# Five pieces for the third table part in nine loads, two table parts fewer held, and another order of the output buffers

## The chip, the cores and the metric

The kernel runs on one core of one Trainium2 chip. The metric is the device time of one execution in microseconds (us), as the median of several runs. The profile is one execution recorded by the hardware profiler. Its engines are PE (matrix products, with PEld for its weight loads), DVE (vector), ACT (scalar), POOL (gathers) and SP (which here only issues transfers). Sixteen DMA engines carry every transfer, each transfer cut into shares for several of them.

## The reference, cut to what matters

```python
emb = emb_table.at[0].set(0.0)            # 100001 x 128, float32
e = emb[seq]                              # seq: 1024 x 50
prefix = jnp.cumsum(e, axis=1)
denom = jnp.minimum(t_idx[None, :], lengths[:, None])
uF = prefix / denom[:, :, None]
y = (uF - uF.mean(axis=0)) * lax.rsqrt(uF.var(axis=0) + BN_EPS) * gamma + beta
def step(v, x):                           # over the 50 time steps
    v = v + (x - v) / TAU                 # TAU = 2
    spike = (v - V_TH >= 0)               # V_TH = 1
    return v - spike * V_TH, spike
uF_out = spikes.mean(axis=0)              # 1024 x 128
scores = uF_out @ emb.T                   # 1024 x 100001
```

The output holds 1024 × 100,001 floats, 409.6 MB. That is most of what moves.

## The kernel before, in words

**First stage.** POOL gathers 1024 rows of the table for each of the 50 steps with eight indirect DMAs (line L207). PE turns them into a prefix sum in PSUM, DVE and ACT normalise it and step the neuron, and the spikes are counted. Beside this, SP loads the first 40 parts of the table into on-chip memory. A *part* is 1024 table rows; the table has 98, the last with 673 rows. A part lies as 128 partitions of eight table rows, 4 KB to a partition. The number of parts held from the first stage is `held`: 36 in six groups of six (`rows0` to `rows5`), two more in the places of the first two once those have been split, and two more in a tile of their own, `spare` with the tag `aside`.

**Second stage.** The score matrix is made in column chunks. `WIDTHS` gives the chunks' widths in parts: four of 2, four of 3, thirteen of 6. For each chunk `c` and each of eight blocks `n` of 128 output rows (`NB = 8`), every part of the chunk is multiplied: `product` (L160) makes four matrix products for a part, of the spike counts with a high and a low half of the table part, into one of four PSUM tiles. The *eviction* copies the product into an output tile `o`, by DVE (L499) and ACT (L501) in turn, scaled by 1/50. When a block is full, `store` (L169) issues one DMA on SP's queue, 1 MB for a chunk of 2, 3 MB for one of 6.

**Splitting.** `prepare` turns a part on PE (L136, eight transposes), casts the high half on ACT (L152) and subtracts on DVE (L153). It needs a free pair of places (`hi`, `lo`), and `ready()` calls it when one is free: once after each block from the third on (from the first in chunk 8), and after each part of a chunk's last block, when that part's pair comes free. Two pairs exist from the first stage; a third comes from the tile `aside` once four parts are split; three each come from groups 0 and 1 when they are used up, and two more from a tile at chunk 8.

**Output buffers.** A list `turns` says which places output tiles take in rotation. At chunks 0, 4 (`NARROW`) and 8 (`MIDDLE`) the pool `op` of output tiles is closed and opened anew, with four, three and three places. From chunk 8 one place is in the new pool and two are the used-up groups `rows2` and `rows3`, in this order:

```python
turns = [(op, "o", 6), (rowp, "rows2", 6), (rowp, "rows3", 6)]
```

A tile in a reused place waits for the last user of that memory, which for an output tile means the landing of the store that read it. The name of a tile is `o_c_n`, so `o_8_0` is the first block of the first wide chunk.

The very first two output tiles, `o_0_0` and `o_0_1` (L428, L430), are made before the pool `op` opens and take places of the first stage: of the gathers and of the tile `rlen`. Chunk 0's later blocks use `op`, which is laid over the memory of the first stage.

**Loads of the second stage.** Parts from number `held` on are fetched on ACT's queue, three at a time, after blocks 1 and 4 of the chunks from 8 on, in group places `rows4` and `rows5` in turn (`fetch`, L109). A load of three parts is one DMA of 128 partitions × 3 × 4 KB. The last part has 84 partitions of eight rows and one more row: two DMAs (L120, L125), with a small memset on DVE.

The order of work on every engine is the order in which the program is written; nothing reorders it.

Of the kernel before, what the change touches and what calls it, by code (L numbers as in the profile page):

```python
# [12 lines left out]
F32 = mybir.dt.float32  # L13
BF16 = mybir.dt.bfloat16
F32R = mybir.dt.float32r
# [5 lines left out]
P = 128  # L21
BN_EPS = 1e-5
V_TH = 1.0
HALF = 1024
KQ = HALF // P
BANK = 512
GROUP = 6
AHEAD = 6
ONLY = 5
TWICE = 2  # L30
ASIDE = 2
SHIFT = TWICE + ASIDE
FURTHER = {5: 1, 6: 2}

WIDTHS = 4 * [2] + 4 * [3] + 13 * [6]
NARROW, MIDDLE = 4, 8


@with_exitstack
def rec_kernel(  # L40
# [9 lines left out]
    nc = tc.nc  # L50
    B, T = seq.shape
    N, D = table.shape
    NB = B // P
# [8 lines left out]


    rowp = ctx.enter_context(tc.tile_pool(name="rows", bufs=1))
    beside = ExitStack()
    asidep = beside.enter_context(tc.tile_pool(name="aside", bufs=1))


    countA = const.tile([P, P], F32R, tag="countA", name="countA")
# [5 lines left out]
    ident = const.tile([P, P], F32, tag="ident", name="ident")  # L75
# [2 lines left out]

    parts = -(-N // HALF)
    assert sum(WIDTHS) == parts  # L80
    held = AHEAD * GROUP + SHIFT
    rows = {}
    split = {}

    free = []
# [4 lines left out]
    def size(q):  # L90
        return min(HALF, N - q * HALF)

    def deep(q):
        return -(-size(q) // KQ)

    def group(g):
        at = g if g < AHEAD else AHEAD - 2 + g % 2
        r = rowp.tile([P, GROUP, HALF], F32, tag=f"rows{at}", name=f"rows_{g}")
        for k in range(GROUP):
            rows[g * GROUP + SHIFT + k if g else k + ASIDE * (k >= TWICE)] = r[:, k, :]  # L100
        return r

    def fetch(r, k, q, n):

        engine = nc.sync if q < held else nc.scalar
        n = min(n, parts - q)
        whole = n - (size(q + n - 1) < HALF)
        if whole:
            engine.dma_start(  # L109
                out=r[:, k : k + whole, :],  # L110
                in_=table[q * HALF : (q + whole) * HALF, :].rearrange("(q p k) d -> p q (k d)", p=P, k=KQ),
            )
        if whole < n:
            full, rest = divmod(size(parts - 1), KQ)
            c1 = (parts - 1) * HALF
            r = r[:, k + whole, :]
            if rest:
                at = full - full % 32
                nc.vector.memset(r[at : at + 32, :], 0.0)
                engine.dma_start(  # L120
                    out=r[full : full + 1, : rest * D],
                    in_=table[c1 + full * KQ : N, :].rearrange("(o k) d -> o (k d)", o=1),
                )
            if full:
                engine.dma_start(  # L125
                    out=r[:full, :],
                    in_=table[c1 : c1 + full * KQ, :].rearrange("(p k) d -> p (k d)", k=KQ),
                )

    def turned(q, pt):  # L130
        r = rows.pop(q)
        if q == 0:
            nc.vector.memset(r[0:1, :D], 0.0)
        pw = deep(q)
        for k0 in range(0, HALF, P):
            nc.tensor.transpose(pt[:, k0 : k0 + pw], r[:pw, k0 : k0 + D], ident[:pw, :pw])  # L136

    def views(q, pt, hi, lo):
        pw = deep(q)
        return (  # L140
            pt.rearrange("d (k p) -> d p k", k=KQ)[:, :pw, :],
            hi[:, : pw * KQ].rearrange("d (p k) -> d p k", k=KQ),
            lo[:, : pw * KQ].rearrange("d (p k) -> d p k", k=KQ),
        )


# [1 line left out]
    def prepare(q, pt):  # L148
        turned(q, pt)
        split[q] = hi, lo = free.pop(0)  # L150
        vp, vh, vl = views(q, pt, hi, lo)
        nc.scalar.copy(vh, vp)  # L152
        nc.vector.tensor_tensor(vl, vp, vh.bitcast(F32), ALU.subtract)  # L153
# [18 lines left out]
    with ExitStack() as ph:  # L172
        once = ph.enter_context(tc.tile_pool(name="once", bufs=1))
        lp = ph.enter_context(tc.tile_pool(name="lif", bufs=1))
        sp = ph.enter_context(tc.tile_pool(name="stats", bufs=3))
        up = ph.enter_context(tc.tile_pool(name="uF", bufs=1))
        gp = ph.enter_context(tc.tile_pool(name="gather", bufs=2))
        accp = ph.enter_context(tc.tile_pool(name="acc", bufs=1, space=bass.MemoryType.PSUM))
        vp = ph.enter_context(tc.tile_pool(name="v", bufs=1, space=bass.MemoryType.PSUM))
# [8 lines left out]
        nc.sync.dma_start(out=gb[:, 0:1], in_=gamma.rearrange("(d o) -> d o", o=1))  # L188
        nc.sync.dma_start(out=gb[:, 1:2], in_=beta.rearrange("(d o) -> d o", o=1))
        first = group(0)  # L190
        fetch(first, 0, 0, TWICE)
        spare = asidep.tile([P, ASIDE, HALF], F32, tag="aside", name="spare")
        for k in range(ASIDE):
            rows[TWICE + k] = spare[:, k, :]
        fetch(spare, 0, TWICE, ASIDE)
        fetch(first, TWICE, SHIFT, GROUP - TWICE)
        for g in range(1, AHEAD):
            fetch(group(g), 0, g * GROUP + SHIFT, GROUP)

# [107 lines left out]
        for t in range(T):  # L309
# [69 lines left out]
            if not last:  # L379
                vt = vp.tile([P, B], F32, tag=f"v{t % 2}", name=f"v_{t}")  # L380
                x(vt, whole)
                if t:
                    spiked(count, whole, v)
                step(vt, whole)
                v = vt
                d = over(t, v)
                if t + 2 < T:
                    l = only(t + 2)

                if t in (T - 8, T - 6):  # L390
                    q = (t - T + 8) // 2
                    pair(q)
                    prepare(q, vp.tile([P, HALF], F32, tag="v1", name=f"pt_{q}"))
                    if q == TWICE - 1:
                        for k in range(TWICE):
                            rows[GROUP + ASIDE + k] = first[:, k, :]
                        nc.sync.dma_start(
                            out=first[:, :TWICE, :],
                            in_=table[(GROUP + ASIDE) * HALF : (GROUP + SHIFT) * HALF, :].rearrange(
                                "(q p k) d -> p q (k d)", p=P, k=KQ  # L400
                            ),
                        )
# [16 lines left out]

        po0 = accp.tile([P, HALF], F32, tag="po0", name="po_0_0")  # L420
        po1 = vp.tile([P, HALF], F32, tag="v0", name="po_0_1")
        for q, (pool, tag, po) in enumerate(((gp, "e", po0), (once, "rlen", po1))):
            o = pool.tile([P, HALF], F32, tag=tag, name=f"o_0_{q}")
            for h, cs in enumerate(halves):
                product(po[:, cs], q, 0, h * BANK, BANK)
            for h, cs in enumerate(halves):
                if q and h:
                    nc.vector.tensor_scalar_mul(o[:, cs], po[:, cs], 1.0 / T)  # L428
                else:
                    nc.scalar.mul(o[:, cs], po[:, cs], 1.0 / T)  # L430
                store(0, q * HALF + h * BANK, o[:, cs])
# [10 lines left out]
    q0 = 0  # L442
    to_split = WIDTHS[0]
    to_fetch = held
    third = None

    def places(at):
        t = rowp.tile([P, GROUP, HALF], F32R, tag=f"rows{at}", name=f"pairs_{at}")
# [2 lines left out]
    for c, W in enumerate(WIDTHS):  # L451

        if c in (0, NARROW, MIDDLE):
            opening.close()
            if c == NARROW:
                assert third in free
                free.remove(third)
                beside.close()
            where = opening if c < MIDDLE else ctx
            op = where.enter_context(tc.tile_pool(name="o", bufs=1, reuse_waits="tile"))  # L460
            if c == 0:
                turns = [(op, f"o{k}", 2) for k in range(4)]
            elif c == NARROW:
                turns = [(op, f"o{k}", 3) for k in (2, 0, 1)]
            else:
                fourth = op.tile([P, 4, HALF], F32R, tag="pairs", name="pairs")
                free.extend((fourth[:, k, :], fourth[:, k + 1, :]) for k in (0, 2))
                turns = [(op, "o", 6), (rowp, "rows2", 6), (rowp, "rows3", 6)]
            blocks = 0
        q1 = q0 + W  # L470
        q2 = q1 + (WIDTHS[c + 1] if c + 1 < len(WIDTHS) else 0)

        def ready():
            nonlocal to_split, third
            if to_split < q2 + FURTHER.get(c, 0) and free:
                prepare(to_split, psum.tile([P, HALF], F32, tag="ps", name=f"pt_{to_split}"))
                to_split += 1

                if to_split == SHIFT:
                    t = asidep.tile([P, ASIDE, HALF], F32R, tag="aside", name="third")  # L480
                    third = (t[:, 0, :], t[:, 1, :])
                    free.append(third)
                if to_split in (GROUP + SHIFT, 2 * GROUP + SHIFT):
                    places(to_split // GROUP - 1)

        for n in range(NB):
# [20 lines left out]
                    ready()  # L507
            if c or n > 1:
                store(n, q0 * HALF, o[:, : min(N, q1 * HALF) - q0 * HALF])
            if (2 if c != MIDDLE else 0) <= n < NB - 1:  # L510
                ready()

            if n in (1, 4) and c >= MIDDLE and to_fetch < parts:
                g, k = divmod(to_fetch - SHIFT, GROUP)
                if k or to_split >= (g - 1) * GROUP + SHIFT:
                    if k == 0:
                        r = group(g)
                    fetch(r, k, to_fetch, GROUP // 2)
                    to_fetch += GROUP // 2
        assert to_split >= q2  # L520
        q0 = q1


# [17 lines left out]
```

## Time and profile before

| what | value |
|---|---|
| median of 3 runs | 1586.12 us (1585.55 to 1586.83) |
| the profiled execution's own time | 1586.83 us |
| its span | 1584.6 us |
| mean granted clock of PE | 0.947 |
| busy: PE, DVE, ACT, POOL | 71%, 60%, 42%, 25% of the span |
| hardware DMA queue q1 (SP) | 430.86 MB, 64.7% of 16 engines' span |
| hardware DMA queue q10 (ACT) | 30.23 MB, 4.7% |
| gathers (L207) | 400, 959 ns each on POOL |
| evictions | 391 on DVE at 1221 ns, 391 on ACT at 1020 ns |
| split of a part | cast on ACT 1008 ns, subtraction on DVE 1217 ns |

The span is the time from the first to the last recorded work; the execution's own time is 2.2 us longer. The gathers end near 515 us, and the second stage takes the rest. A page of the profile has the busy shares in 40 slices of 39.6 us, each digit a tenth; the traffic of the DMA engines in GB/s; and the chain of waits that ended last, with each step's share of the span. In the list of waits a row says which engine and line waited for whom, for how long in total, how often, and the longest. In the timeline a bracket at the end gives the idle time before an instruction and what ended it. The issue rows give the DMAs of a kind, their size, and the median time from issue to landing.

### The profile page before, as it was taken

To read this page: it belongs to the slowest core of one execution; us is meant where nothing else is said; L and a number is where in the kernel's file an instruction comes from. 1 tells how busy PE (TensorE), PEld (TensorE's weight loads), DVE (VectorE), ACT (ScalarE), POOL (GpSimd) and SP (SyncE) were. 2 spreads that over 40 slices of the span, in tenths; PEclk is the share of its full clock that TensorE was granted. 3 is DMA by queue.
4 is the path that set the end of the run, shared out by engine and by line. 5 is a ranking of instruction groups with operands and counts; after the bars stand their busy time and mean duration, and the time that the engine had idled before them with its cause. 6 is when DMAs were issued, how large, how long until landed. Compare 5 with 4: busy or idle time off the path is not lost.

```text
span 1584.6 us, 12233 instructions
## 1 busy us (share of the span) xinstructions
PE 1129.8 (71%) x4452; PEld 801.0 (51%) x4452; DVE 946.1 (60%) x1124; ACT 668.9 (42%) x697; POOL 389.0 (25%) x408
## 2 busy tenths in 40 slices
PE   4544444444444988897988888887888787888884
PEld 2211111111122766676766666666666666666663
DVE  5777677777777566565655555555555545555552
ACT  2333333333333554554544444444444444444542
POOL 7777777777777000000000000000000000000000
PEclk9999999999995999999999999998999999999997
DMA  9711111111121899997999999999999999999998
GB/s 348 259 53 52 52 53 52 53 52 53 51 79 46 343 415 406 423 415 313 428 425 426 431 429 427 427 425 426 414 425 418 426 427 418 416 416 429 427 401 343
DMA packets 51313, 488.12 MB, mean 308 GB/s; under 512 B 10079, under 2 KB 10336, under 8 KB 30004
## 3 DMA queue, kind: packets, MB, share of 16 engines
q1 hardware_dynamic: 30752, 430.86, 64.7%
q0 software_dynamic: 12800, 26.24, 5.7%
q10 hardware_dynamic: 7700, 30.23, 4.7%
q8 instruction: 35, 0.57, 0.1%
q14 instruction: 26, 0.21, 0.0%
HBM read 77.69 MB, written 409.60 MB: 308 GB/s over the span
## 4 chain that ended last, share of the span: by engine, by line
DMA 55%; POOL 18%; PE 11%; issue 8%; ACT 5%; DVE 2%; ACTq 0%; POOLq 0%; DVEq 0%; SPq 0%
DMA scores<-o 47%; POOL e L207 18%; PE po L160 10%; DMA e<-in_L_rec_emb_table,idx 7%; ACT o L501 5%; DVE o L499 1%; PE pt L136 1%; PE pre L320 0%; ACT pairs L152 0%; DMA idx<-in_r_seq 0%; DVE pairs L153 0%; ACTq L501 0%; DVE uF L329 0%; DVE centred L347 0%; ACT o L430 0%
## 5 line engine op out<-in xcount | busy, mean ns | idle before, releaser
L499 DVE TENSOR_SCALAR o<-po 128x1024 f32<-128x1024 f32 x391 | 464.5, 1221 | 348.1 <-DMA scores<-o 311.1
L501 ACT ACTIVATE o<-po 128x1024 f32<-128x1024 f32 (+1 forms) x391 | 389.5, 1020 | 546.7 <-DMA scores<-o 325.5
L207 POOL DMA_INDIRECT e<-in_L_rec_emb_table,idx x400 | 383.4, 959 | 123.9 <-issue 109.4
L320 PE MATMUL pre<-ident,e 128*128 128x128 f32 x400 | 180.4, 464 | 232.5 <-DMA e<-in_L_rec_emb_table,idx 232.0
L160 PE MATMUL po<-pairs,countB 128*128 128x512 f32 (+1 forms) x1120 | 296.5, 411 | 63.4 <-ACT o L501 48.6
L160 PEld LDWEIGHTS po<-pairs,countB 128*128 128x128 f32 x1120 | 213.3, 196 | 125.9 <-ACT o L501 65.0
L160 PE MATMUL po<-pairs,countC 128*128 128x512 f32 (+1 forms) x840 | 231.2, 423 | 45.8 <-ACT o L501 45.6
L320 PEld LDWEIGHTS pre<-ident,e 128*128 128x128 f32 x400 | 73.5, 184 | 342.8 <-DMA e<-in_L_rec_emb_table,idx 342.1
L160 PEld LDWEIGHTS po<-pairs,countC 128*128 128x128 f32 x840 | 165.2, 203 | 92.1 <-ACT o L501 57.0
L153 DVE TENSOR_TENSOR pairs<-pt,pairs 128x1024 fp32r<-128x1024 f32 x70 | 84.6, 1217 | 93.3 <-ACT pairs L152 93.3
L329 DVE SCALAR_TENSOR_TENSOR uF<-rlen,pre 128x512 f32<-128x512 f32 x100 | 68.4, 684 | 113.4 <-PE pre L320 113.3
L136 PE MATMUL pt<-ident,rows 128*128 128x128 f32 (+1 forms) x768 | 110.8, 292 | 9.9 <-issue 4.9
L136 PEld LDWEIGHTS pt<-ident,rows 128*128 128x128 f32 (+1 forms) x768 | 100.6, 154 | 28.1 <-issue 12.7
L344 ACT ACTIVATE r<-mv,eps 128x1 f32<-128x1 f32 x50 | 14.8, 297 | 227.2 <-DVE mv L340 227.2
L160 PE MATMUL po<-hi,countB 128*128 128x512 f32 x208 | 86.0, 413 | 16.6 <-ACT o L501 11.3
L281 PE MATMUL pre<-zT,ls 128*128 128x512 f32 x100 | 78.1, 783 | 22.7 <-DVE uF L329 18.8
L160 PE MATMUL po<-lo,countB 128*128 128x512 f32 x208 | 83.2, 400 | 0.0
L160 PE MATMUL po<-pairs,countA 128*128 128x512 f32 x280 | 71.3, 401 | 15.0 <-ACT o L501 15.0
L293 ACT ACTIVATE d<-v,less 128x1024 bf16<-128x1024 f32 x49 | 54.7, 1116 | 63.5 <-DVE v L377 63.5
L152 ACT CAST pairs<-pt 128x1024 fp32r<-128x1024 f32 x70 | 70.6, 1008 | 16.2 <-PE pt L136 16.1
L160 PE MATMUL po<-hi,countC 128*128 128x512 f32 x156 | 65.4, 419 | 13.7 <-ACT o L501 13.5
L374 ACT ACTIVATE v<-uF,hgb,a 128x1024 f32<-128x1024 f32 x49 | 59.3, 1210 | 30.4 <-DVE a L370 30.4
(87 smaller groups left out, 850.3 us busy)
## 6 DMA issues: line engine op xcount, KB each, us to landing
scores<-o SPq DMA_DIRECT2D x96, 3072.0 KB, 20.1
scores<-o SPq DMA_DIRECT2D x32, 1536.0 KB, 8.9
scores<-o SPq DMA_DIRECT2D x30, 1024.0 KB, 8.6
rows<-in_L_rec_emb_table ACTq DMA_DIRECT2D x19, 1536.0 KB, 29.0
scores<-o SPq DMA_DIRECT2D x8, 2896.5 KB, 17.4
rows<-in_L_rec_emb_table SPq DMA_DIRECT2D x5, 3072.0 KB, 34.7
e<-in_L_rec_emb_table,idx POOLq DMA_INDIRECT x400, 2.5
rows<-in_L_rec_emb_table SPq DMA_DIRECT2D x2, 1024.0 KB
```

The source lines that it names most:

```text
L136: nc.tensor.transpose(pt[:, k0 : k0 + pw], r[:pw, k0 : k0 + D], ident[:pw, :pw])
L152: nc.scalar.copy(vh, vp)
L153: nc.vector.tensor_tensor(vl, vp, vh.bitcast(F32), ALU.subtract)
L160: nc.tensor.matmul(po[:, :kw], lhsT=counts[n], rhs=part[:, k0 : k0 + kw], start=j == 0, stop=j == 1,)
L207: nc.gpsimd.indirect_dma_start(out=es[t][:, n * P : (n + 1) * P], out_offset=None, in_=table, in_offset=bass.IndirectOffsetOnAxis(ap=idx[: ...
L281: nc.tensor.matmul(pre[h], lhsT=l, rhs=zT[:, h * BANK : (h + 1) * BANK], start=t == 0, stop=False, skip_group_check=True,)
L293: nc.scalar.activation(d, v, AF.Identity, bias=less)
L320: nc.tensor.matmul(pre[h][:, k : k + P], lhsT=e[:, h * BANK + k : h * BANK + k + P], rhs=ident, start=False, stop=last, is_transpose=True, ...
L329: nc.vector.scalar_tensor_tensor(uF[:, cs], rlen[:, cs], 1.0 / (t + 1), pre[h], ALU.max, ALU.mult)
L374: nc.scalar.activation(vt, uF[:, cs], AF.Identity, bias=hgb[:, 1:2], scale=a)
L499: nc.vector.tensor_scalar_mul(o[:, h0 : h0 + hw], po[:, :hw], 1.0 / T)
L501: nc.scalar.mul(o[:, h0 : h0 + hw], po[:, :hw], 1.0 / T)
```

## The change

1. **Two parts fewer are held.** The tile `aside` is dropped, `held` is 38 and not 40, and 60 parts in place of 58 are fetched in the second stage. The third pair (`hi2`, `lo2`) is in the output pool from chunk 0 to chunk 3.
2. **Pool `uF` has two buffers** and `o_0_1` takes one of them, not the place of `rlen`.
3. **Five DMAs for a part.** In loads number 0, 2, ... 16 of the second stage (`FEWER`, nine loads) the third part comes in five DMAs of 16, 35, 35, 21 and 21 partitions (`PIECES`), issued ahead of one DMA for the first two parts. In the other loads the three parts come in one DMA, as before.
4. **The last part** is laid out with one table row to a partition: one DMA of 128 partitions × 5 × 512 B and one of 33 partitions × 512 B, 673 rows. Its split and transposes follow that layout.
5. **The order of the output places from chunk 8** is `rows2`, `rows3`, then the new pool's place.
6. **`ready()`** runs after the third block at the earliest in every chunk, and never splits a part beyond the next chunk's.

```diff
-ASIDE = 2
-SHIFT = TWICE + ASIDE
-FURTHER = {5: 1, 6: 2}
+FEWER = range(0, 18, 2)
+PIECES = (16, 35, 35, 21, 21)
...
-    held = AHEAD * GROUP + SHIFT
+    held = AHEAD * GROUP + TWICE
...
+        if (q - held) // (GROUP // 2) in FEWER:
+            whole -= 1
+            n = whole
+            one = r[:, k + whole, :]
+            src = table[(q + whole) * HALF : (q + whole + 1) * HALF, :].rearrange("(p k) d -> p (k d)", k=KQ)
+            p0 = 0
+            for pw in PIECES:
+                engine.dma_start(out=one[p0 : p0 + pw, :], in_=src[p0 : p0 + pw, :])
+                p0 += pw
...
-            full, rest = divmod(size(parts - 1), KQ)
+            full, rest = divmod(size(parts - 1), P)
...
+                    out=r[:, :full, :],
+                    in_=table[c1 : c1 + full * P, :].rearrange("(k p) d -> p k d", p=P),
...
+            if rest:
+                engine.dma_start(out=r[:rest, full, :], in_=table[c1 + full * P : N, :])
...
-        up = ph.enter_context(tc.tile_pool(name="uF", bufs=1))
+        up = ph.enter_context(tc.tile_pool(name="uF", bufs=2))
...
-        for q, (pool, tag, po) in enumerate(((gp, "e", po0), (once, "rlen", po1))):
+        for q, (pool, tag, po) in enumerate(((gp, "e", po0), (up, "uF", po1))):
...
+                third = [op.tile([P, HALF], F32R, tag=x, name=x) for x in ("hi2", "lo2")]
+                free.append(third)
...
-                turns = [(op, "o", 6), (rowp, "rows2", 6), (rowp, "rows3", 6)]
+                turns = [(rowp, "rows2", 6), (rowp, "rows3", 6), (op, "o", 6)]
...
-            if to_split < q2 + FURTHER.get(c, 0) and free:
+            if to_split < q2 and free:
...
-                if to_split == SHIFT:
-                    t = asidep.tile([P, ASIDE, HALF], F32R, tag="aside", name="third")
-                    third = (t[:, 0, :], t[:, 1, :])
-                    free.append(third)
...
-            if (2 if c != MIDDLE else 0) <= n < NB - 1:
+            if 2 <= n < NB - 1:
```

More of the change, by code (lines that the diff above doesn't have):

```diff
@@ L64, in rec_kernel @@
     rowp = ctx.enter_context(tc.tile_pool(name="rows", bufs=1))
-    beside = ExitStack()
-    asidep = beside.enter_context(tc.tile_pool(name="aside", bufs=1))
     countA = const.tile([P, P], F32R, tag="countA", name="countA")
@@ L91, in size @@
         return min(HALF, N - q * HALF)
-    def deep(q):
-        return -(-size(q) // KQ)
     def group(g):
@@ L99, in group, with fetch @@
         for k in range(GROUP):
-            rows[g * GROUP + SHIFT + k if g else k + ASIDE * (k >= TWICE)] = r[:, k, :]
+            rows[g * GROUP + (TWICE if g else 0) + k] = r[:, k, :]
         return r
-    def fetch(r, k, q, n):
+    def fetch(r, q, n):
         engine = nc.sync if q < held else nc.scalar
+        k = q if q < GROUP else (q - TWICE) % GROUP
         n = min(n, parts - q)
         whole = n - (size(q + n - 1) < HALF)
+        if (q - held) // (GROUP // 2) in FEWER:
[7 more added lines that the diff above has]
+                p0 += pw
+            assert p0 == P
         if whole:
@@ L113, in fetch @@
         if whole < n:
-            full, rest = divmod(size(parts - 1), KQ)
+            full, rest = divmod(size(parts - 1), P)
             c1 = (parts - 1) * HALF
[L116 to L123, printed above, removed]
+            r = r[:, k + whole, :].rearrange("p (k d) -> p k d", d=D)
             if full:
                 engine.dma_start(
-                    out=r[:full, :],
-                    in_=table[c1 : c1 + full * KQ, :].rearrange("(p k) d -> p (k d)", k=KQ),
-                )
+                    out=r[:, :full, :],
+                    in_=table[c1 : c1 + full * P, :].rearrange("(k p) d -> p k d", p=P),
+                )
+            if rest:
+                engine.dma_start(out=r[:rest, full, :], in_=table[c1 + full * P : N, :])
     def turned(q, pt):
@@ L133, in turned @@
             nc.vector.memset(r[0:1, :D], 0.0)
-        pw = deep(q)
-        for k0 in range(0, HALF, P):
-            nc.tensor.transpose(pt[:, k0 : k0 + pw], r[:pw, k0 : k0 + D], ident[:pw, :pw])
+        for k0 in range(0, size(q), P):
+            kw = min(P, size(q) - k0)
+            nc.tensor.transpose(pt[:, k0 : k0 + kw], r[:kw, k0 : k0 + D], ident[:kw, :kw])
     def views(q, pt, hi, lo):
-        pw = deep(q)
+        hw = size(q)
+        if hw < HALF:
+            return pt[:, :hw], hi[:, :hw], lo[:, :hw]
         return (
-            pt.rearrange("d (k p) -> d p k", k=KQ)[:, :pw, :],
-            hi[:, : pw * KQ].rearrange("d (p k) -> d p k", k=KQ),
-            lo[:, : pw * KQ].rearrange("d (p k) -> d p k", k=KQ),
+            pt.rearrange("d (k p) -> d p k", k=KQ),
+            hi.rearrange("d (p k) -> d p k", k=KQ),
+            lo.rearrange("d (p k) -> d p k", k=KQ),
         )
@@ L150, in prepare @@
         split[q] = hi, lo = free.pop(0)
+        hw = size(q)
+        if hw % 2:
+            nc.vector.memset(hi[:, hw : hw + 1].bitcast(F32), 0.0)
+            nc.vector.memset(lo[:, hw : hw + 1].bitcast(F32), 0.0)
         vp, vh, vl = views(q, pt, hi, lo)
@@ L190, in rec_kernel @@
         first = group(0)
[L191 to L196, printed above, removed]
+        fetch(first, 0, GROUP)
         for g in range(1, AHEAD):
-            fetch(group(g), 0, g * GROUP + SHIFT, GROUP)
+            fetch(group(g), g * GROUP + TWICE, GROUP)
         es = {}
@@ L395, in rec_kernel @@
                         for k in range(TWICE):
-                            rows[GROUP + ASIDE + k] = first[:, k, :]
+                            rows[GROUP + k] = first[:, k, :]
                         nc.sync.dma_start(
                             out=first[:, :TWICE, :],
-                            in_=table[(GROUP + ASIDE) * HALF : (GROUP + SHIFT) * HALF, :].rearrange(
+                            in_=table[GROUP * HALF : (GROUP + TWICE) * HALF, :].rearrange(
                                 "(q p k) d -> p q (k d)", p=P, k=KQ
@@ L444, in rec_kernel @@
     to_fetch = held
-    third = None
     def places(at):
@@ L454, in rec_kernel @@
             opening.close()
[L455 to L458, printed above, removed]
             where = opening if c < MIDDLE else ctx
@@ L461, in rec_kernel @@
             if c == 0:
+                third = [op.tile([P, HALF], F32R, tag=x, name=x) for x in ("hi2", "lo2")]
+                free.append(third)
                 turns = [(op, f"o{k}", 2) for k in range(4)]
             elif c == NARROW:
+                assert third in free
+                free.remove(third)
                 turns = [(op, f"o{k}", 3) for k in (2, 0, 1)]
@@ L473, in ready @@
         def ready():
-            nonlocal to_split, third
-            if to_split < q2 + FURTHER.get(c, 0) and free:
+            nonlocal to_split
+            if to_split < q2 and free:
                 prepare(to_split, psum.tile([P, HALF], F32, tag="ps", name=f"pt_{to_split}"))
                 to_split += 1
-                if to_split == SHIFT:
-                    t = asidep.tile([P, ASIDE, HALF], F32R, tag="aside", name="third")
-                    third = (t[:, 0, :], t[:, 1, :])
-                    free.append(third)
-                if to_split in (GROUP + SHIFT, 2 * GROUP + SHIFT):
+                if to_split in (GROUP + TWICE, 2 * GROUP + TWICE):
                     places(to_split // GROUP - 1)
@@ L509, in rec_kernel @@
                 store(n, q0 * HALF, o[:, : min(N, q1 * HALF) - q0 * HALF])
-            if (2 if c != MIDDLE else 0) <= n < NB - 1:
+            if 2 <= n < NB - 1:
                 ready()
             if n in (1, 4) and c >= MIDDLE and to_fetch < parts:
-                g, k = divmod(to_fetch - SHIFT, GROUP)
-                if k or to_split >= (g - 1) * GROUP + SHIFT:
+                g, k = divmod(to_fetch - TWICE, GROUP)
+                if k or to_split >= (g - 1) * GROUP + TWICE:
                     if k == 0:
                         r = group(g)
-                    fetch(r, k, to_fetch, GROUP // 2)
+                    fetch(r, to_fetch, GROUP // 2)
                     to_fetch += GROUP // 2
-        assert to_split >= q2
+        assert to_split == q2
         q0 = q1
```

## The prediction

> **What bounds the kernel now.** I read the page first: its 40 slices, then its chain.
>
> ```profile
> PEclk9999999999995999999999999998999999999997
> DMA  9711111111121899997999999999999999999998
> GB/s 348 259 53 52 52 53 52 53 52 53 51 79 46 343 415 406 423 415 313 428 425 426 431 429 427 427 425 426 414 425 418 426 427 418 416 416 429 427 401 343
> ...
> DMA 55%; POOL 18%; PE 11%; issue 8%; ACT 5%; DVE 2%; ACTq 0%; POOLq 0%; DVEq 0%; SPq 0%
> ```
>
> A slice is 39.6 us. Through slice 12 the gathers set the pace and DMA is nearly idle; from slice 13 (515 us) the DMA engines are full at some 425 GB/s and the chain is mostly their work. One slice falls out: 313 GB/s at 713 to 752 us. So the windows, finer (columns: stretch, length, busy us of PE, PEld, DVE, ACT, POOL, granted clock, DMA share, GB/s):
>
> ```profile
> 720.00:740.00 20.00, 13.49 (x51) 10.85 (x52) 8.83 (x9) 6.04 (x6) 0.00 (x0) 0.83 0.49 207
> 760.00:815.00 55.00, 48.91 (x232) 39.26 (x230) 33.04 (x28) 28.22 (x29) 0.00 (x0) 1.00 1.01 429
> ...
> 1110.00:1160.00 50.00, 42.13 (x183) 33.20 (x182) 26.90 (x23) 22.20 (x23) 0.00 (x0) 0.94 1.00 417
> ```
>
> In 20 us at 720 the DMA engines are half idle; elsewhere full, a little slower where a table load is under way. Who waits there: the waits of 716 to 736 us, then the timeline, then the waits of 515 to 530 us.
>
> ```profile
> ACT o L501 <- DMA scores<-o: 11.3, 2, 8.5
> DVE o L499 <- DMA scores<-o: 7.1, 1, 7.1
> ```
>
> ```profile
> 728.43 1.94 ACT L501 ACTIVATE o<-po 128x1024 f32<-128x1024 f32 x2 [8.51 <-DMA scores<-o]
> ```
>
> ```profile
> ACT o L501 <- DMA scores<-o: 3.5, 1, 3.5
> ...
> DVE o L499 <- DMA scores<-o: 2.6, 1, 2.6
> ```
>
> The evictions of o_8_0, the first of the wide chunks, stand still until the last narrow store has landed, so nothing is queued when it has.
>
> The last view is the packet records of the 16 DMA engines after 735 us. A store's 24,576-byte packet takes 912 ns (median), a load's 4,096-byte packet 159 ns. One engine takes 933 to 946 and 164 to 173 ns. Its share of each store lands last, by 0.2 us at 743 us, 7.5 us at 1003 us, 7 to 9.5 us from there on; at the end the others are done at 1576.3 us and it at 1583.2 us. It is never idle from 735.2 to 1583.2 us: 848 us, where its packets at the others' times make 827.3. So 20.7 us of its time are excess, and the others lose 20.7 − 7 = 13.7 us to waiting for it. This engine bounds the second stage.
>
> **The change, part by part.** Sums run in time of the profiled execution: span 1584.6 us, its own time 1586.83, 0.7 above the median 1586.12. The last packet ends at 1583.2, so a run's median is that end + 2.9.
>
> *Opening.* o_0_1 takes a second uF buffer, so the evictions of row block 1 no longer wait for its stores' landing (3.5 and 2.6 us above). Block 2 waits instead, later. The stores are back to back from about 530.05 instead of 531.5 us: −1.45 us, bounds 0 (the stall goes to block 2) and −2.4.
>
> *Start of the wide chunks.* o_8_0 and o_8_1 go into the rows places, free of stores; the third block, o_8_2, gets the place that waits, its landing long past. The first wide store is issued at about 726.2 us, not 734.48. The hole of 720 to 740 us costs the engines 10.7 us of idle time on average; it shrinks by the 8.2 us between these issues, by 7.4 for the late engine, whose queue empties later. Bounds −6 and −10.7 (the whole hole). What is late next is the 1.22-us and 1.02-us evictions, six to a store, which need less time than its 7.3 us of transfer.
>
> *Two parts fewer held.* They are fetched in the second stage: 2 × 128 packets of 4 KB over 16 engines = 16 × 0.162 us (mean of this packet) = +2.6 us each; by bytes, 1.05 MB at 428 GB/s = +2.45. In the first stage they go beside the gathers (POOL busy 389 us, 75% of it), worth 0.
>
> *Last part.* It comes as 673 packets of 512 B, 43 on the fullest engine. The one 512-B packet there now took 33 ns: 1.4 us against 6 × 0.159 = 0.95: +0.4, bounds 0 and +1.
>
> *Third pair, order of ready().* Evictions, products and splits are the same in number (PE 1719 rows of program to 1736, DVE 1125 to 1126). Their cover is the store: a wide block's six products are 5.5 us on PE and its six evictions 3.7 us on DVE and 3.1 on ACT, under 7.3 us. Worth 0; without cover, a split's 1.0 + 1.2 us once a part.
>
> *Five pieces in nine loads.* Six issues replace one: 45 more on ACT's queue at 0.37 to 0.47 us, so 1.9 to 2.3 us ahead of the evictions behind them, nine times. ACT is busy 42% and one or two stores are queued: 0; with no store queued, nine times 2.1 = +19. SP and POOL's queues are not passed. The load lands a few us later than the 29 us of the issue rows; its first transpose comes 80 us or more after its issue.
>
> What counts is which engines carry the pieces. The trace shows three row counts:
>
> ```profile
> rows<-in_L_rec_emb_table ACTq DMA_DIRECT2D x19, 1536.0 KB, 29.0
> ...
> rows<-in_L_rec_emb_table ACTq DMA_DIRECT2D x1, 336.0 KB
> ...
> rows<-in_L_rec_emb_table ACTq DMA_DIRECT2D x1, 0.5 KB
> ```
>
> The first, 128 rows a part, puts 8 packets of a part on all 16; the second, 84 rows, ran on 14 engines, 6 packets each; the single row on one. 14 is the largest divisor of 84 up to 16. By that, 35 and 21 rows run on 7 engines, 5 and 3 packets each, 16 rows on 16. A part in pieces then puts 1 + 5 + 5 + 3 + 3 = 17 packets on seven engines and 1 on nine, instead of 8 on each: +9 × 0.162 = +1.46 us, and −7 × 0.162 = −1.13. Times nine: **+13.1 us on seven, −10.2 on nine**.
>
> The Trainium skill (DMA: Bandwidth & Descriptors, "Why a DMA increments its semaphore by 16 and not by 1") has the same divisor rule and adds that the lowest-numbered engines are taken; its "Latency and other measured facts" calls engines 7 and 15 usually the slower ones, with a cause it says is a guess. By these the late one would be engine 7, outside engines 0 to 6; the trace has one such engine, not two. Against the change stands "Rules for kernel authors" of the same page, to use all 16 engines: taken alone, 13.1 us lost. The row of 848 against 827.3 us says why that need not be: the engines are not equal here.
>
> From the rows alone: the late engine is among the 14 of the 84-row load, and is not the one of the single row. If seven of the 14, that one included, carry the pieces, the late one is among them with a chance between 0 (places fixed, it lies outside) and 6 in 13 (places unknown). I take 0.20, a little under the middle, and keep both ends for the range.
>
> *Sum.* The seven: start of the wide stores 735.2 − 1.45 − 8.2 = 725.5; + 827.3 of packets, + 2.6 + 0.4, + 13.1 = 1568.9; + about 3 for waits that stay (24 packets of instruction code of 0.93 us, of which a hit engine's neighbours are stretched to 1.3 to 1.5 us, and 2.0 us of idle at 1510 to 1515 us): 1572. The late engine: 735.2 − 1.45 − 7.4 = 726.3; + 848 + 2.6 + 0.4 − 10.2 = 1567. The seven end last, at 1572; + 2.9 = **1575 us**, 11 less. Bounds of the unknowns: −1.45 −8.2 could be −2.4 −10.7 or 0 −6, and the 3 us of waits 0 to 7: 1568.5 to 1582.5.
>
> **The rivals.**
> 1. *The hole closes, the pieces even out nothing*: the late engine's lag is not worked off by fewer load packets. 1583.2 − 1.45 − 7.4 + 3.0 + 2.9 = 1580.2. For: the excess sits in its 768 store packets (768 × 21 to 34 ns = 16 to 26 us). Against: its lag is a queue of bytes of any kind, and it is never idle. Chance 0.12.
> 2. *The change does not do what it says at the wide chunks*: the hole only moves to o_8_2, or to the split of the next part. Then the seven end 8.2 later: 1583. For: ACT and DVE also prepare parts there. Against: three places, two of them free. Chance 0.06; inside the measurement's doubt.
> 3. *Slower: the late engine is one of the seven.* It gets +13.1 instead of −10.2: 726.3 + 848 + 3.0 + 13.1 = 1590.4, + 2.9 = 1593.3. It decides from the engine's place alone, nothing else need go wrong; it turns from gain to loss at 5.9 / 1.46 = 4 such loads. For: no record numbers the engines of the coming pieces. Against: only the single row's engine, one fewer of the seven. Chance 0.20.
>
> **How the numbers follow.** The forecast has 0.62. About 0.2% (3.2 us) is what a measurement of this kernel can tell from no change, so faster is below 1582.9: forecast and rival 1, less 0.02 of their tails, 0.72; same 0.08; slower 0.20. The range leaves out rival 3 and takes the forecast's bounds and rivals 1 and 2: 1568 to 1587.
>
> **What would show it.** Right: the slice at 713 us above 400 GB/s and no wait on scores<-o of over 3 us by o_8_0; issue rows of 64, 140 and 84 KB on ACT's queue, the last two on seven engines; stores whose late share trails by 1 to 4 us, no longer 7 to 9, with several engines instead of one last; ACT's waits unchanged. Wrong: the late engine inside the seven, its lag growing by more than 1 us at each of the nine loads; DMA share under 0.95 in the windows of the loads; or evictions behind the issues that come after the previous store has ended.

## The result and the profile after

The changed kernel takes 1591.79 us (median of 6 runs, 1591.22 to 1592.29) where the kernel before took 1586.09 (6 runs beside it): ratio 1.0036, 95% interval 1.0023 to 1.0049. It is 5.7 us slower; 1575 had been forecast, 1568 to 1587 the range. The profiled execution took 1591.93 us with a span of 1589.8.

The page after, in the order in which the lines of before were shown:

```profile
DMA  9611111111121999999999999999999999999998
GB/s 348 230 53 53 51 53 53 51 54 53 52 80 41 385 416 405 423 416 404 424 427 413 431 398 404 422 415 431 398 413 415 405 427 392 431 419 425 400 421 351
...
DMA 55%; POOL 18%; PE 10%; issue 8%; ACT 5%; DVE 2%; another core or an unknown queue 1%; ACTq 0%; SPq 0%; POOLq 0%; DVEq 0%
```

Slice 18 has risen from 313 to 404 GB/s: the hole at the start of the wide chunks is closed. But dips that were not there stand all along the rest: 413, 398, 404, 398, 405, 392. The windows show both, first the one that was a hole, then three places where a load in pieces is under way (stretch, length, busy us of PE, PEld, DVE, ACT, POOL, granted clock, DMA share, GB/s):

```profile
720.00:740.00 20.00, 20.00 (x95) 16.61 (x94) 14.51 (x13) 11.31 (x13) 0.00 (x0) 1.00 0.97 414
```

```profile
910.00:930.00 20.00, 16.52 (x64) 12.86 (x63) 8.09 (x7) 6.42 (x7) 0.00 (x0) 0.83 0.91 376
980.00:1000.00 20.00, 14.50 (x60) 11.24 (x59) 7.16 (x7) 7.52 (x8) 0.00 (x0) 0.91 0.88 364
1120.00:1140.00 20.00, 15.31 (x61) 10.82 (x59) 9.39 (x8) 7.81 (x9) 0.00 (x0) 0.91 0.90 366
```

At 720 us the share went from 0.49 to 0.97. In each of the three others an engine is idle for a tenth of the time on average. Summed from the packet records, the 16 engines are idle for 17 us each (mean) between 740 and 1515 us, where it was 4.4 before. The waits of 716 to 736 us no longer name the stores:

```profile
ACT o L497 <- PE po L166: 7.6, 9, 1.3
DVE o L495 <- PE po L166: 3.8, 7, 0.6
```

The issue rows have the pieces, and the timeline of ACT what their issue takes:

```profile
rows<-in_L_rec_emb_table ACTq DMA_DIRECT2D x18, 140.0 KB
rows<-in_L_rec_emb_table ACTq DMA_DIRECT2D x18, 84.0 KB
...
rows<-in_L_rec_emb_table ACTq DMA_DIRECT2D x9, 64.0 KB
```

```profile
782.40 5.55 ACTq L110 DMA_DIRECT2D rows<-in_L_rec_emb_table  x5
787.98 1.28 ACTq L114 DMA_DIRECT2D rows<-in_L_rec_emb_table  x1
789.44 2.86 ACT L497 ACTIVATE o<-po 128x1024 f32<-128x1024 f32 x3 [6.02 <-PE po L166]
```

Where the pieces run is in the landing records (us after the issue, one number for each record), here of most of the fourth load in pieces and, in the last row, of the last piece of the seventh:

```
988.59, 16 rows: 4.8 5.9 5.9 5.9 5.9 6.0 6.0 6.0 6.0 6.0 6.0 6.1 6.2 6.3 6.5 6.9
990.20, 35 rows: 1.4 8.6 9.5 9.6 9.6 10.6 14.8 16.3
992.69, 21 rows: 1.4 14.3 14.6 14.7 14.7 15.5 19.8 21.1
...
1199.62, 21 rows: 0.8 12.1 12.3 12.4 12.4 12.4 12.4 20.5
```

The first piece has 16 records. A piece of 35 or 21 rows has eight: one early (at 1.4 us, where the first share of data of this load comes at 4.8) and seven shares, so it runs on seven engines, as forecast. But the last share of the last piece comes 6.4 us after the first four have landed (21.1 against 14.7); in the second to the ninth load this gap is 3.8 to 9.1 us, in the first, when the late engine has hardly fallen back, 0.1. The row of 1199.62 us shows it most plainly: six shares within 0.3 us, and one 8.1 us behind them. So the record points to **the late engine being one of the seven**; the experiments have to show that this is what costs. The last store packet ends at 1588.09 us, 863.6 us after the first wide one; the third rival had 1590.4, 864.1 after its start at 726.3. (One more packet, of instruction code, ends at 1591.96, after the last instruction.)

### The profile page after: what moved, and what is told of

It is laid out like the page before. It is cut to its first block, busy times and chain, and to the rows that moved or that the text cites. A ratio compares the mean times of both kernels' runs of the same rounds, so it can differ in the third digit from the quotient of the medians.

```text
span 1589.8 us, 12311 instructions
## 1 busy us (share of the span) xinstructions
PE 1134.7 (71%) x4450; PEld 800.2 (50%) x4450; DVE 945.4 (59%) x1125; ACT 667.1 (42%) x697; POOL 387.9 (24%) x408
## 4 chain that ended last, share of the span: by engine, by line
DMA 55%; POOL 18%; PE 10%; issue 8%; ACT 5%; DVE 2%; another core or an unknown queue 1%; ACTq 0%; SPq 0%; POOLq 0%; DVEq 0%
DMA scores<-o 49%; POOL e L208 18%; PE po L166 9%; DMA e<-in_L_rec_emb_table,idx 5%; ACT o L497 4%; DVE o L495 1%; ACT pairs L158 0%; PE pt L136 0%; PE pre L321 0%; DVE pairs L159 0%; DMA idx<-in_r_seq 0%; DVE uF L330 0%; DVE bs L331 0%; ACTq L497 0%
## 5 line engine op out<-in xcount | busy, mean ns | idle before, releaser
L166 PE MATMUL po<-pairs,countB 128*128 128x512 f32 x1136 | 309.6, 419 | 64.1 <-ACT o L497 57.2
L166 PEld LDWEIGHTS po<-pairs,countB 128*128 128x128 f32 x1136 | 221.3, 200 | 130.6 <-ACT o L497 71.0
L166 PE MATMUL po<-pairs,countC 128*128 128x512 f32 x852 | 238.5, 427 | 52.9 <-ACT o L497 52.9
L166 PEld LDWEIGHTS po<-pairs,countC 128*128 128x128 f32 x852 | 168.4, 204 | 99.5 <-ACT o L497 64.5
L136 PE MATMUL pt<-ident,rows 128*128 128x128 f32 x782 | 107.8, 283 | 11.0 <-issue 4.9
L136 PEld LDWEIGHTS pt<-ident,rows 128*128 128x128 f32 x782 | 96.1, 147 | 30.5 <-issue 10.9
L166 PE MATMUL po<-hi,countB 128*128 128x512 f32 x216 | 89.4, 414 | 17.8 <-ACT o L497 13.4
L166 PE MATMUL po<-hi,countC 128*128 128x512 f32 (+1 forms) x162 | 67.4, 416 | 14.6 <-ACT o L497 14.6
L158 ACT CAST pairs<-pt 128x1024 fp32r<-128x1024 f32 x71 | 72.0, 1014 | 10.2 <-PE pt L136 10.0
```

Source lines behind the costliest of these rows:

```text
L136: nc.tensor.transpose(pt[:, k0 : k0 + kw], r[:kw, k0 : k0 + D], ident[:kw, :kw])
L166: nc.tensor.matmul(po[:, :kw], lhsT=counts[n], rhs=part[:, k0 : k0 + kw], start=j == 0, stop=j == 1,)
```

## The experiments

They ran on three other chips, where the stage of the gathers takes some 60 us longer, so each is compared with the kernel before on its own chip. Beside the ratio I give the *wide stage*: from the first 24,576-byte store packet to the end of the last store packet, of the profiled execution. It does not see the first stage. In four profiles of the kernel without pieces, on three chips, it was 851.4 to 851.8 us, so a difference of 1 us tells. The kernel before was profiled on the first chip only.

| kernel | median, us | before beside it | ratio (95%) | wide stage, us |
|---|---|---|---|---|
| before, after (first chip) | 1586.09, 1591.79 | | 1.0036 (1.0023 to 1.0049) | 848.0, 863.6 |
| no_pieces | 1641.84 | 1649.23 | 0.9948 (0.9930 to 0.9966) | 851.6 |
| pieces_only | 1661.28 | 1649.23 | 1.0068 (1.0047 to 1.0088) | 860.1 |
| which | 1643.83 | 1649.23 | 0.9959 (0.9939 to 0.9979) | 853.4 |
| old_turns | 1649.51 | 1649.23 | 0.9998 (0.9985 to 1.0011) | 850.0 |
| after_again | 1652.45 | 1644.96 | 1.0043 (1.0030 to 1.0056) | 863.6 |
| no_pieces_2 | 1638.45 | 1644.96 | 0.9959 (0.9947 to 0.9972) | 851.4 |
| four_loads | 1644.68 | 1644.96 | 0.9998 (0.9986 to 1.0011) | 857.2 |
| fives | 1650.54 | 1644.96 | 1.0032 (1.0019 to 1.0044) | 863.0 |
| on_four | 1637.32 | 1645.58 | 0.9951 (0.9934 to 0.9968) | 851.2 |
| on_three | 1640.22 | 1645.58 | 0.9955 (0.9938 to 0.9971) | 853.5 |
| on_two | 1645.39 | 1645.58 | 0.9992 (0.9973 to 1.0010) | 855.1 |
| no_pieces_3 | 1639.16 | 1645.58 | 0.9960 (0.9942 to 0.9977) | 851.8 |
| fives_2 | 1654.38 | 1649.59 | 1.0024 (1.0008 to 1.0039) | 862.9 |
| on_four_2 | 1641.31 | 1649.59 | 0.9952 (0.9932 to 0.9972) | 850.0 |
| spread_four | 1646.01 | 1649.59 | 0.9981 (0.9964 to 0.9999) | 855.8 |
| no_pieces_4 | 1641.80 | 1649.59 | 0.9958 (0.9935 to 0.9981) | 851.6 |

**The pieces taken out, and the pieces alone.**

```diff
 no_pieces (changed kernel):
-FEWER = range(0, 18, 2)
+FEWER = ()
 pieces_only (kernel before):
+        if q >= held and (q - held) // (GROUP // 2) in FEWER:
+            ... the five DMAs of the change ...
```

> The changed kernel with no load split into pieces (every load of three parts is one DMA on all engines); the rest of the change stays. Theory A (the late DMA engine is one of the seven that carry the pieces, so they lengthen the work of the engine that bounds): the loss goes and the other parts' gain is left, 1586.1 - 1.45 - 7.4 + 3.0 = 1580 us, 1577 to 1582. Theory B (the pieces are harmless or help; the loss is in the other parts: two more parts fetched, the last part in 512-byte rows, the order of the output places): 1590 us or more.

> The kernel before with the five pieces in the third part of loads 0, 2, ... 16 and nothing else of the change. Theory A: 9 x 9 packets of 0.162 us more on the bounding engine, 1586.1 + 13.1 = 1599 us, 1595 to 1601. Theory B: 1586 or less; with the late engine outside the seven some 1578 to 1583 us.

(The absolute times in the expectations were for the first chip.) Without the pieces the change is 7.4 us faster than the kernel before (medians); the pieces alone make the kernel before 12.1 us slower, and the wide stage 860.1 where it was 848.0 on the first chip. So the loss is the pieces', as theory A has it, and it is about the 13.1 us of packets. That it is the late engine's packets, and not the issues of the pieces, these two runs do not tell apart.

**The order of the output places.**

```diff
 old_turns (no_pieces, and):
-                turns = [(rowp, "rows2", 6), (rowp, "rows3", 6), (op, "o", 6)]
+                turns = [(op, "o", 6), (rowp, "rows2", 6), (rowp, "rows3", 6)]
```

> The changed kernel without pieces and with the order of the output places of before (op, rows2, rows3). Both theories: the hole at the start of the wide chunks comes back, + 7.4 us against the kernel without pieces, so 1587 us under A (bounds +6 to +10.7). If the hole's end is worth nothing, no difference.

7.7 us slower than without the edit, so the order of the places is worth what was forecast. What is left of the change in this kernel (the opening, two more parts, the last part) makes no difference to before: 0.9998.

**The price by the number of loads, on one chip.**

```diff
 four_loads (changed kernel):
-FEWER = range(0, 18, 2)
+FEWER = range(0, 16, 4)
```

> The changed kernel as it is, beside the same without pieces on one chip. Theory A: + 13.1 us against the kernel without pieces (nine loads of 9 packets more on the late engine), 11 to 15.

> The changed kernel without pieces, again. Both theories: 0.995 of the kernel before, as measured first.

> Pieces of 16, 35, 35, 21, 21 rows in four loads (0, 4, 8, 12) in place of nine. Theory A: the price goes with the packets on the late engine, 4 x 1.46 = + 5.8 us against the kernel without pieces, so about the time of the kernel before less 2. If the pieces cost by what they delay (issues on ACT's queue, a load that lands too late) and not by packets, the four may cost nothing or as much as the nine.

Nine loads cost 14.0 us by the medians and 12.2 in the wide stage, four 6.2 and 5.8: 1.4 to 1.6 us a load, against 1.46 from the packets. The cost goes with the number of loads in pieces; as packets and issues grow alike with it, it does not say which of them costs. Four loads give back just what the rest of the change gains, as the third rival had it.

**Which engine it is.**

```diff
 which (changed kernel):
-PIECES = (16, 35, 35, 21, 21)
+PIECES = (1, 2, 3, 4, 5, 6, 11, 96)
```

> The changed kernel with other pieces: 1, 2, 3, 4, 5, 6, 11 and 96 rows, so that a piece of k rows has one packet on each of k engines. Theory A: the pieces' landings show from which k on one share trails the others by over 2 us; that k less 1 is the late engine's place s, and it is under 7. The late engine carries 13 - s packets of such a part (7 at s = 6) in place of 8, so the time is that of the kernel without pieces + 9 x 0.162 x (5 - s): +7.3 us for s = 0, 0 for s = 5, -1.5 for s = 6. Theory B: no piece of up to 6 rows has a share that trails.

This one misled me by its landings and helped by its time. In all nine loads the last share of the 6-row piece trails those of the 5-row piece by 0.5 to 2.0 us, from which I took the sixth engine for the late one. But the last share of *every* small piece comes late (5.9, 7.3, 8.3, 7.4, 6.5, 7.2 us after the issue for 1 to 6 rows in the first load). My reading, not tested, is that it belongs to the engine that has just joined, where it stands behind store packets. The wide stage is 1.8 us longer than without pieces (medians: 2.0); 1.46 x (5 − s) gives s = 3.8 (3.6), nearer to the fifth engine (s = 4) than to the sixth.

The run settles something else. Its nine issues for a load hold ACT up longer than the six of the change: in the first load ACT is idle for 11.7 us behind them, against 6.0.

```profile
850.82 8.65 ACTq L110 DMA_DIRECT2D rows<-in_L_rec_emb_table  x8
863.00 0.40 ACTq L114 DMA_DIRECT2D rows<-in_L_rec_emb_table  x1
863.52 2.85 ACT L497 ACTIVATE o<-po 128x1024 f32<-128x1024 f32 x3 [11.68 <-DMA scores<-o]
```

Yet nine such loads cost 2 us and not 12 to 14. So the issues are not what the change loses by.

```diff
 fives, fives_2:
+FEWER = range(0, 14, 2);  PIECES = (48, 25, 25, 25, 5)
 on_four, on_four_2:
+FEWER = range(0, 10, 2);  PIECES = (48, 76, 4)
 on_three:
+FEWER = range(0, 6, 2);  PIECES = (32, 93, 3)
 on_two:
+FEWER = range(0, 6, 2);  PIECES = (64, 62, 2)
```

> Pieces of 48, 25, 25, 25 and 5 rows in seven loads (0, 2, ... 12): the last four run on five engines only, which leaves the sixth out. If the sixth engine is the late one (theory A as the pieces of 1 to 6 rows showed it): it carries 3 packets of such a part, not 8, 7 x 5 x 0.162 = -5.7 us; the first five get 19, + 12.5 us on engines that stand some 18 us better: 4 to 6 us faster than the kernel without pieces. If the late one is among the first five, + 12 us; if pieces cost in themselves, slower too.

> Pieces of 48, 76 and 4 rows in five loads: 76 = 4 x 19 and 4 rows run on four engines, 23 packets of such a part on each of these, 3 on the twelve others. The late engine is in the first five by the run of the fives. If it is the fifth: 5 x 5 x 0.162 = -4.1 us on it against the kernel without pieces, + 12.2 on the four, which have room: -2 to -4 us. If it is one of the first four: + 12.2 us.

> Pieces of 32, 93 and 3 rows in three loads: three engines get 34 packets of such a part, the others 2. Against the kernel without pieces: -2.9 us if the late engine is the fourth or fifth, + 12.6 us if it is one of the first three.

> Pieces of 64, 62 and 2 rows in three loads: two engines get 36 packets of such a part, the others 4. Against the kernel without pieces: -1.9 us if the late engine is the third, fourth or fifth, + 13.6 us if it is one of the first two.

> The changed kernel without pieces, on the same chip as the three above: 0.995 to 0.996 of the kernel before.

The fives cost 12.1 us, not a gain: the late engine is one of the five. The same 12 us of packets on four engines cost nothing (0.9951 against 0.9960, wide stage 0.6 us shorter), so it is none of the four. The forecast gain of 2 to 4 us did not come either. The pieces on three and on two meet neither of their forecasts, but lie far from + 12.6 and + 13.6 (wide stage + 1.7 and + 3.3). With two, 36 packets on two engines in one load leave the other fourteen dry: all sixteen are idle for a mean 3.0 and 3.2 us at 950 and 1020 us.

Fives and fours had run on two chips, so both again on one:

> The pieces on five engines in seven loads again, now on one chip with the pieces on four. If the fifth engine is the late one here too: + 12.5 us against the kernel without pieces. If what costs is the packets taken up by any few engines, on_four on the same chip costs as much.

> The pieces on four engines in five loads again, 12.2 us more on each of the four. If the fifth is the late one: -2 to -4 us against the kernel without pieces. If what costs is packets on any few engines: + 12 us as with five.

> The changed kernel without pieces, on the same chip as the three above: 0.995 to 0.996 of the kernel before.

The wide stage is 11.3 us longer with fives than without pieces, and 1.6 us shorter with fours. An equal load costs all or nothing by whether it runs on five engines or on four.

The landing records of the last piece say the same (the clearest load with five, and one with four):

```
fives_2, 988.05, 5 rows: 1.4 13.1 13.1 13.2 14.0 23.5
on_four_2, 1119.64, 4 rows: 1.3 26.8 26.8 26.9 27.0
```

With five engines the last share is 3.1 to 9.5 us behind the one before it in four of fourteen loads; with four it is at most 1.1 us behind in all ten. So the five hold the late engine and the four do not. That it is *the fifth* adds that the four are among the five. No record numbers the engines; the time of `which` agrees. (On the first chip only "one of the seven" is shown.)

**A version that follows from it.**

```diff
 spread_four:
+FEWER = range(18);  PIECES = (112, 4, 4, 4, 4)
```

> Pieces of 112, 4, 4, 4 and 4 rows in eighteen loads: 11 packets of such a part on four engines, 7 on the others, so 18 x 0.162 = -2.9 us on the late engine in small steps, + 8.7 on the four. If the fifth is the late one: 2 to 3 us faster than the kernel without pieces. If it is one of the four: + 8.7 us.

It missed: 4.2 us slower than without pieces. Its waits from 800 to 1600 us have a row that the kernel without pieces does not have among its costliest, and the timeline of ACT shows one place of it:

```profile
ACT o L497 <- issue: 86.8, 12, 13.1
```

```profile
870.97 8.59 ACTq L110 DMA_DIRECT2D rows<-in_L_rec_emb_table  x5
879.59 1.26 ACTq L114 DMA_DIRECT2D rows<-in_L_rec_emb_table  x1
881.03 2.85 ACT L497 ACTIVATE o<-po 128x1024 f32<-128x1024 f32 x3 [9.05 <-DMA rows<-in_L_rec_emb_table]
```

With a load in pieces after blocks 1 and 4 of every chunk, the last small piece of every second load is issued 4 to 8 us after the one before it is done, and ACT stands for 9 to 13 us. That this makes the 4.2 us was not tested, and `which` speaks against taking it as given: ACT stood for 10 to 12 us there too, in nine loads, for a loss of 2 us. The late engine's lag did shrink: its share of the last store trails the middle one by 2.6 us, where it was 4.1 and 6.1 in the two profiles without pieces on this chip.

The best kernel is the changed one without pieces, 0.4 to 0.5% faster than before in four measurements; with pieces on four engines it is 0.5% faster too, and the two can't be told apart.

## Why the prediction was wrong, point by point

**The place of the late engine** is the step that failed: "I take 0.20, a little under the middle". The rows of before left it open, up to 6 in 13, and nothing there favoured the outside. The sum then went on with −10.2 us for the late engine, where the runs show + 12 to + 14. The mechanism itself, an engine that bounds the stage and pays for each packet more, was right, and so was the third rival that had it the other way round: with + 13.1 it comes to 1593.3 us; measured 1591.8. One of the prediction's own signs of being wrong came too, a DMA share under 0.95 while the loads run (0.88 to 0.91). I ought to have noticed that the range, cut just below that rival, stood on this one chance of 0.20.

**The sentence on the skill** pulled the same way. Of the Trainium skill (DMA: Bandwidth & Descriptors), the divisor rule ("Why a DMA increments its semaphore by 16 and not by 1") held: 35 and 21 rows ran on 7 engines, 25 on 5, 76 on 4. Its remark that engines 7 and 15 are usually the slower ones ("Latency and other measured facts") does not fit here together with its rule that the lowest-numbered engines are taken: the late engine is among the five of a DMA on five, which by that rule are engines 0 to 4. No record numbers the engines, so which of the two sentences does not fit this chip isn't settled. The rule to use all 16 engines ("Rules for kernel authors") spoke against the change, and keeping to it would have saved the loss; but with pieces on four engines it cost nothing to break it.

**Start of the wide chunks**: right. The first wide packet goes at 724.5 us (725.5 to 726.3 forecast), the share in the hole is 0.97, and the order of the places is worth 7.7 us (7.4).

**Opening, two parts, last part**: the stall of row block 1 is gone from the waits of 515 to 530 us. The three together were to cost 1.55 us; old_turns has −0.3 by its ratio, with some 2 us either way. Each by itself was not measured. In the wide stage old_turns is 2.0 us longer than before, on another chip, where + 3.0 had been forecast. A 512-byte packet took 27 ns, not 33.

**Issues on ACT's queue**: mis-sized. The row of 0.37 to 0.47 us was of issues with none just before them. In a load in pieces the first issue takes 0.33 to 0.39 us and most of those behind it some 1.2; the six take 5.3 to 7.2 us and not some 2.5. It is not the number of engines: L123, on 16 engines and right behind another issue, took 1.27 us, and the 1 row of `which`, on one engine but first in its load, 0.25 to 0.52. What makes the later issues longer stays open. They were hidden all the same: the wide stage grew by 12.1 and 12.2 us, the packets alone ask for 13.1, and `which` cost 2 us with more issues.

**Rival 1**, that fewer load packets do not work off the late engine's lag, is half open. Packets put on the engine cost what the sum said. Packets taken off it (4.1 us in five loads) brought 0.6 and 1.6 us of the wide stage, and in spread_four the lag at the end was 2.6 us, with 4.1 and 6.1 without pieces, and the kernel got slower. So the −10.2 us might not have come in full even with the late engine outside.

## What to carry to other kernels

Here a DMA whose number of rows was not a multiple of 16 ran on as many engines as its largest divisor up to 16 (35 rows on 7, 76 on 4, 93 on 3), and a late share stood among the seven in eight of nine loads. Before steering traffic with that, find out whether the slowest engine is among them, by a run that loads k of them and one that loads k − 1. When all that a forecast's sign rests on is one unknown place, its chance is what the rows leave open, and the range has to reach that side. A change of several parts is taken apart: here a gain of 7 us and a loss of 12 to 14 stood in one diff.

## What the runs showed of the hardware

- One DMA engine of 16 is late on all four chips: in the kernel before and in the four runs without pieces its share of the last store lands 4.0 to 6.9 us after the middle one. In the runs that can tell it is among the five engines of a DMA on five and not among the four of a DMA on four.
- A DMA on k engines under 16 has k + 1 landing records (35 rows: 8; 25 rows: 6; 4 rows: 5), the first of them 0.4 to 2 us after the issue.
- Issues that follow each other at once on ACT's queue in the wide stage took 1.1 to 1.2 us each by the median on fewer than 16 engines (after, which, fives, spread_four; in on_four 0.4) and 1.1 to 1.3 on 16 (the same four), where one with none just before it took 0.25 to 0.5 us.
- The 1-row piece of `which`, issued when the load before it had landed, landed 5.6 to 6.4 us after its issue, with the engines full of stores. After the issue at 905.85 us of on_four, where the engines are idle for 2.2 us of the next 5 on average, the shares of 48 rows landed after 2.2 to 4.6 us.
- In spread_four, where loads in pieces follow each other within some 30 us, the issue itself is held up: 8.59 us for five issues, the last of them 4 us after the one before it.
